# Summing four of eight factor slices by accumulating DMAs in the last two setup steps of a cross-attention and FFN kernel

## The chip, the cores and the metric

The kernel runs on one core of one Trainium2 chip. The metric is the device time of one execution, in microseconds (us); lower is better. The five engines are TensorE (PE in the profile), VectorE (DVE), ScalarE (ACT), GpSimd (POOL) and SyncE (SP); each works through its own queue in order, and they wait for one another by semaphores.

## The reference

The input `x` has 8 sequences of 1024 rows with 1024 elements, all in float32. Each sequence has 64 memory rows and a mask over them. There are eight factor matrices of 1024x1024.

```python
x = x + attention(layernorm(x), memory, mask)      # one head, 64 memory rows per sequence
mixed = einsum('btd,rde->bte', layernorm(x), factors)   # sums over the 8 factors r too
x = x + mixed / sqrt(8) + bias
```

The sum over `r` doesn't depend on `x`, so the eight factors can be added up once, and the second line is then one product with a single 1024x1024 matrix.

## The kernel before

**Work per group.** The 8192 rows are handled in 16 groups of 512 rows. A group's rows are loaded (`load_rows`, L140, and from group 2 on `load_blocks`, L131, for a blocked copy that VectorE transposes), scored against the memory (`scores`, `scores_back`, `softmax`, `weights_back`, `read_out`), added to `x` (`residual`, L292), normalised (`norm_stats`, `normalize`), transposed, and multiplied by the summed factor matrix. A group has two halves `q`, each with seven `unit`s or `product`s: the matrix product is done with seven block products instead of eight, on combined blocks of the rows (`combine_rows`) and of the matrix (`combine_factors`). Each product is four matmuls of 128x512 (L398), and `give` (L411) adds its result to `x`.

**The combined matrix.** The blocks are kept in seven tiles, `b11`, `t2`, `b22`, `b21`, `t1`, `t3`, `t4`. The raw sums are made in `QUADS` order: steps 0 and 1 sum the top half of the matrix into `b11` and `t2`, steps 2 and 3 the bottom half into `b21` and `b22`. `combine_factors` then forms `t1` (steps 0, 1), and `t2`, `t3` (L445, L446) and `t4` (L448) in steps 2 and 3. The units need `b11`, `t1`, `t2`, `b22`, `t3`, `b21`, `t4` in this order, so units 0 and 1 can run after step 1, and unit 2 and all that follow need the whole of steps 2 and 3.

**A step.** One step takes a quarter of each of the eight factors, a slice of 128 partitions by 2048 elements, 1 MB. SP issues the loads (`load_factor`, L428) into tiles of the pool `big`, which has nine buffers of 8 KB per partition. The same pool holds the transposed rows (`xT`, `hT`), the normalised rows (`h`) and the blocked copies (`xb`, `hb`). VectorE adds some of the slices into the block tiles (L540); TensorE adds the others, by multiplying them with the identity into four PSUM banks (`sum_on_pe`, L436), and VectorE adds those banks at the end of the step (L547). In steps 0 and 1 VectorE takes factors 0 to 3 and TensorE 4 to 7; in steps 2 and 3 VectorE takes 0 to 4 and TensorE 5, 6 and 7.

**What runs beside the steps.** `beside(step, turn)` writes out by hand which work of groups 0 and 1 stands between the turns of each step. Around the change these are, in this order: in step 2 the transposes of group 0's second half and `unit(0, 0, 0)`; `unit(0, 0, 1)`; the transposes of group 1 (`transpose_x_pe`, L193 and L194) with `row_sums(1)` (L147 on ScalarE, then `nmean`, L149 on GpSimd); more transposes with `row_squares(1)` (L158 on ScalarE, which needs `nmean`, then L162 and L163 on GpSimd). In step 3 they are `scores(1)`, `scores_back(1)`, `softmax(1)` with `unit(0, 1, 0)`, and `unit(0, 1, 1)`. GpSimd's queue thus holds small arithmetic only, among it L305 to L309 of `norm_stats`. The schedule is the program's order: nothing reorders an engine's queue.

Of the kernel before, what the change touches and what calls it, by code (L numbers as in the profile page):

```python
# [12 lines left out]
ALU = mybir.AluOpType  # L13
# [7 lines left out]
def kernel(  # L21
# [18 lines left out]
    nc = tc.nc  # L40
# [7 lines left out]
    NC = DA // Q  # L48
    KH = NC // 2
    H = D // 2  # L50
# [17 lines left out]
    COMMON = ["ps0", "ps1", "ps2", "ps3"]  # L68
    ring = list(COMMON)

    def bank(name: str, tag: str = ""):
        if not tag:
            ring.append(ring.pop(0))
            tag = ring[-1]
        return psum.tile([P, 512], F32, tag=tag, name=name)

    def big_tile(shape, name: str):
        return big.tile(shape, F32, tag="big", name=name)
# [346 lines left out]
    def load_factor(step: int, r: int):  # L425

        f = big_tile([P, 2, D], f"f_{step}_{r}")
        nc.sync.dma_start(  # L428
            f, factors[r].rearrange("(p c) e -> p c e", c=NC)[:, 2 * step : 2 * step + 2, :]
        )  # L430
        return f

    def sum_on_pe(f, first: bool, last: bool, banks):
        for c in range(2):
            for n in range(2):
                nc.tensor.matmul(banks[c, n], ident, f[:, c, ts(n, H)], start=first, stop=last)  # L436

    def combine_factors(step: int, n: int):

        c = slice(2 * (step % 2), 2 * (step % 2) + 2)  # L440
        w = {key: tile[:, c, :] for key, tile in wq.items()}
        if step < 2 and n == 0:
            nc.vector.tensor_sub(w["t1"], w["t2"], w["b11"])
        if step >= 2 and n == 1:
            nc.vector.tensor_sub(w["t2"], w["b22"], w["t1"])  # L445
            nc.vector.tensor_sub(w["t3"], w["t2"], w["b11"])  # L446
        if step >= 2 and n == 0:
            nc.vector.tensor_sub(w["t4"], w["b21"], w["t2"])  # L448
# [17 lines left out]
    def beside(i: int, s: int):  # L466
        if (i, s) == (0, -1):
            centre_memory(0)
            row_stats(0)
            transpose_x_pe(0, 0)  # L470
            transpose_x_pe(0, 1)
        if (i, s) == (0, 0):
            transpose_memory(0)
            scores(0)
        if (i, s) == (0, 1):
            scores_back(0)
        if (i, s) == (0, 2):
            softmax(0)
            nc.scalar.dma_start(bias_bc, bias.partition_broadcast(P))
        if (i, s) == (0, 3):  # L480
            weights_back(0)
        if (i, s) == (1, 0):
            read_out(0, 0)
            residual(0, 0)
        if (i, s) == (1, 1):
            norm_stats(0, 0)
            read_out(0, 1)
            normalize(0, 0, False)
            residual(0, 1)
        if (i, s) == (1, 2):  # L490
            norm_stats(0, 1)
            transpose_h_pe(0, 0)
            load_rows(1, nc.sync)
        if (i, s) == (1, 3):
            normalize(0, 1, False)
            add_bias(0, 0, nc.vector)
        if (i, s) == (2, 0):
            transpose_h_pe(0, 1)
            combine_rows(0, 0)
            unit(0, 0, 0)  # L500
        if (i, s) == (2, 1):
            unit(0, 0, 1)
            add_bias(0, 1, nc.vector)
        if (i, s) == (2, 2):
            combine_rows(0, 1, (1,))
            transpose_x_pe(1, 0)
            row_sums(1)
        if (i, s) == (2, 3):
            transpose_x_pe(1, 1)
            row_squares(1)  # L510
        if (i, s) == (3, 0):
            scores(1)
        if (i, s) == (3, 1):
            scores_back(1)
        if (i, s) == (3, 2):
            softmax(1)
            unit(0, 1, 0)
        if (i, s) == (3, 3):
            unit(0, 1, 1)

    for step in range(NS):
        c2 = slice(2 * (step % 2), 2 * (step % 2) + 2)
        w2 = [wq[key][:, c2, :] for key in QUADS[step // 2]]

        sums = {(c, n): bank(f"sum_{step}_{c}_{n}", COMMON[2 * c + n]) for c in range(2) for n in range(2)}
        ring[:] = ["u0", "v0", "u1", "v1"] if step < 2 else ["u1", "v1"]
        beside(step, -1)

        turns = [((0,), 4), ((1,), 5), ((2,), 6), ((3,), 7)]
        if step >= 2:  # L530
            turns = [((0, 1), None), ((2,), 5), ((3,), 6), ((4,), 7)]
        before = None
        for s, (mine, other) in enumerate(turns):
            for r in mine:
                f = load_factor(step, r)
                if r == 0:
                    before = f
                    continue
                for n, w in enumerate(w2):
                    nc.vector.tensor_add(w, before[:, :, ts(n, H)] if r == 1 else w, f[:, :, ts(n, H)])  # L540
            if other is not None:
                fp = load_factor(step, other)
                sum_on_pe(fp, other == turns[1][1] - (step < 2), other == 7, sums)
            beside(step, s)
        for n in (1, 0):
            for c in range(2):
                nc.vector.tensor_add(w2[n][:, c, :], sums[c, n], w2[n][:, c, :])  # L547
            combine_factors(step, n)
    ring[:] = COMMON

# [42 lines left out]
    for g in range(1, NG):  # L593
        n, m = g + 1, g + 2
# [91 lines left out]
```

## Time and profile before

| | us |
|---|---|
| median of 3 runs | 1019.69 |
| lowest and highest | 1014.05 and 1020.04 |
| the profiled execution | 1018.94 |
| its span, first to last instruction | 1016.6 |
| TensorE busy | 985.7 |
| VectorE busy | 669.3 |
| ScalarE busy | 349.6 |
| GpSimd busy | 215.8 |

The profile covers one execution. Times in its views are counted from the start of the span. A line such as L436 is a line of the kernel file before the change. A float32 matmul is recorded as two entries, so four matmuls show as x8. The chain of waits gives, for each piece, its start, its length, and what it is; the chain is followed back from the last instruction. In the windows each engine has its busy time and count, then come TensorE's clock, DMA's share of the 16 engines and GB/s. The bracket at the end of a timeline row tells how long the engine was idle ahead of it and what ended that.

### The profile page before, as it was taken

Reading aid. Unit: us, or ns where it says so; the run is one execution under the profiler, and the core shown is the slowest. Engines: PE = TensorE matmul, PEld = TensorE weight load, DVE = VectorE, ACT = ScalarE, POOL = GpSimd, SP = SyncE. Lnnn points to the kernel's source line nnn. Section 1 sums busy time; section 2 is a strip of 40 time slices with the busy share of each in tenths; the row PEclk is TensorE's granted clock in tenths of the full one; section 3 lists DMA queues with packets and bytes.
Section 4 is the critical chain, followed back from the end, with each engine's and each line's share of the span. In section 5 each row is a group of like instructions: output and inputs, shape, how many; then the busy total and the mean of one; then the engine's idle time right before and its main releaser. Section 6 shows DMA issues by size and latency. Waiting matters only on the chain.

```text
span 1016.6 us, 8902 instructions
## 1 busy us (share of the span) xinstructions
PE 985.7 (97%) x2896; PEld 443.4 (44%) x2896; DVE 669.3 (66%) x895; ACT 349.6 (34%) x521; POOL 215.8 (21%) x250
## 2 busy tenths in 40 slices
PE   4979999999999999999999999999999999999998
PEld 3445344444444444444444444444444444444443
DVE  3598577675758575675758575675758575695531
ACT  2135134432625143432625143432625143430300
POOL 0020012222213040222213040222213040240400
PEclk9999999999999999999999999999999999999999
DMA  9996936455573937455573837356573837340321
GB/s 320 418 407 267 285 88 164 144 138 149 143 210 95 229 99 166 138 144 143 145 207 95 213 116 171 133 142 146 142 209 92 213 120 171 131 123 32 90 85 41
DMA packets 93517, 166.86 MB, mean 164 GB/s; under 512 B 12320, under 2 KB 71840, under 8 KB 89376
## 3 DMA queue, kind: packets, MB, share of 16 engines
q1 hardware_dynamic: 93024, 165.20, 56.6%
q10 hardware_dynamic: 448, 1.11, 0.4%
q8 instruction: 22, 0.36, 0.1%
q14 instruction: 23, 0.19, 0.1%
HBM read 101.25 MB, written 33.55 MB: 133 GB/s over the span
## 4 chain that ended last, share of the span: by engine, by line
PE 93%; DVE 2%; DMA 2%; ACT 1%; POOL 1%; issue 0%; ACTq 0%
PE yu L398 43%; PE yv L398 22%; PE yz L398 11%; PE ro L281 6%; PE scT L218 5%; PE sum L436 4%; DMA f<-in_L_ffn_factors_dram 2%; PE memTp L120 1%; DVE st L302 1%; DMA mask_raw<-in_mask_BxS_bk_dram 1%; PE tp L193 1%; DVE x L292 0%; ACT junk L158 0%; ACT h L321 0%; PE eTp L269 0%
## 5 line engine op out<-in xcount | busy, mean ns | idle before, releaser
L398 PE MATMUL yu<-t,hT 128*128 128x512 f32 x512 | 232.2, 596 | 0.0
L321 ACT ACTIVATE h<-x,nb,rstd 128x1024 f32<-128x1024 f32 x64 | 137.4, 2198 | 233.0 <-POOL nb L309 167.8
L411 DVE SCALAR_TENSOR_TENSOR x<-yu,x 128x512 f32<-128x512 f32 x128 | 88.0, 687 | 161.8 <-PE yu L398 161.7
L398 PEld LDWEIGHTS yu<-t,hT 128*128 128x128 f32 x512 | 96.5, 191 | 117.0 <-issue 116.2
L333 POOL TENSOR_TENSOR x<-x,bias_bc 128x1024 f32<-128x1024 f32 x60 | 141.8, 2388 | 0.0
L398 PE MATMUL yz<-b,hT 128*128 128x512 f32 x256 | 117.2, 600 | 0.0
L398 PE MATMUL yu<-t,s 128*128 128x512 f32 x256 | 115.4, 593 | 1.5 <-DVE t L445 1.5
L398 PE MATMUL yu<-b,hT 128*128 128x512 f32 x256 | 116.5, 598 | 0.0
L398 PE MATMUL yv<-t,s 128*128 128x512 f32 x256 | 116.5, 598 | 0.0
L398 PE MATMUL yv<-b,s 128*128 128x512 f32 x256 | 115.1, 592 | 0.0
L182 DVE STREAM_TRANSPOSE xT<-xb 128x2048 f32<-128x2048 f32 x28 | 109.8, 3922 | 0.0
L411 DVE SCALAR_TENSOR_TENSOR x<-yv,x 128x512 f32<-128x512 f32 x64 | 43.8, 684 | 93.7 <-PE yv L398 93.7
L292 DVE SCALAR_TENSOR_TENSOR x<-ro,rden,x 128x512 f32<-128x512 f32 x128 | 87.2, 744 | 13.5 <-PE ro L281 13.5
L149 POOL TENSOR_SCALAR nmean<-sum 128x4 f32<-128x4 f32 x15 | 3.6, 237 | 397.9 <-ACT junk L147 397.9
L302 DVE BATCH_NORM_STATS2 st<-x 128x6 f32<-128x512 f32 x128 | 80.3, 669 | 0.0
L398 PEld LDWEIGHTS yu<-b,hT 128*128 128x128 f32 x256 | 47.4, 190 | 64.7 <-issue 64.2
L398 PEld LDWEIGHTS yv<-b,s 128*128 128x128 f32 x256 | 48.6, 190 | 60.7 <-issue 60.5
L398 PEld LDWEIGHTS yz<-b,hT 128*128 128x128 f32 x256 | 47.0, 190 | 63.4 <-issue 51.7
L398 PEld LDWEIGHTS yv<-t,s 128*128 128x128 f32 x256 | 47.5, 190 | 59.9 <-issue 57.6
L398 PEld LDWEIGHTS yu<-t,s 128*128 128x128 f32 x256 | 47.5, 190 | 56.4 <-issue 54.0
L347 DVE STREAM_TRANSPOSE hT<-hb 128x1024 f32<-128x1024 f32 x60 | 70.9, 1219 | 0.2
L158 ACT ACTIVATE junk<-x,nmean 128x1024 f32<-128x1024 f32 x60 | 68.8, 1147 | 1.5
(72 smaller groups left out, 783.7 us busy)
## 6 DMA issues: line engine op xcount, KB each, us to landing
x<-in_x_dram SPq DMA_DIRECT2D x64, 512.0 KB, 10.3
f<-in_L_ffn_factors_dram SPq DMA_DIRECT2D x32, 1024.0 KB, 12.0
out_dram<-x SPq DMA_DIRECT2D x64, 512.0 KB, 2.9
hb<-h SPq DMA_DIRECT2D x480, 64.0 KB, 2.0
xb<-in_x_dram SPq DMA_DIRECT2D x112, 256.0 KB, 7.8
mem<-in_ctx_dram SPq DMA_DIRECT2D x14, 256.0 KB, 3.9
mem<-in_ctx_dram ACTq DMA_DIRECT2D x2, 256.0 KB, 10.3
bias_bc<-in_L_ffn_bias_dram ACTq DMA_DIRECT2D x1, 512.0 KB, 8.1
```

Of the source, the lines that this page charges most:

```text
L158: nc.scalar.activation(junk, st["x", g, t], AF.Square, bias=nmean[:, t : t + 1], accum_out=ss[:, t : t + 1])
L182: nc.vector.transpose(xT.rearrange("p c (t j) -> p t c j", j=Q), xb.rearrange("p t (i c) -> p t c i", i=Q))
L218: nc.tensor.matmul(ps[ts(h, M), : 2 * P], mT[:, c, :], st["xb", g, h][:, c, :], start=(c == 0), stop=(c == NC - 1),)
L281: nc.tensor.matmul(ps, eT[ts(h, M), q, :], m[ts(h, M), ts(n, H)], start=True, stop=True)
L292: nc.vector.scalar_tensor_tensor(xt, st.pop(("ro", g, q, n, h)), rden[:, k : k + 1], xt, ALU.mult, ALU.add)
L302: nc.vector.bn_stats(stats[:, n, :], xt[:, ts(n, H)])
L321: nc.scalar.activation(dst, src, AF.Identity, bias=nb[:, h : h + 1], scale=rstd[:, h : h + 1],)
L333: eng.tensor_add(xt, xt, bias_bc)
L347: nc.vector.transpose(hT[:, h].rearrange("p c (t j) -> p t c j", j=Q), hb[:, h].rearrange("p t (c i) -> p t c i", i=Q),)
L398: nc.tensor.matmul(ps, lhs[:, c, :], wq[rhs][:, c, :], start=(first and c == 0), stop=(c == KH - 1), skip_group_check=True,)
L411: nc.vector.scalar_tensor_tensor(xt, st["y", g, q, key], ISR, xt, ALU.mult, ALU.add)
L436: nc.tensor.matmul(banks[c, n], ident, f[:, c, ts(n, H)], start=first, stop=last)
```

## The change

In steps 2 and 3 SP first loads factor 4 into a tile. GpSimd issues three DMAs that add factors 5, 6 and 7 to that tile in place, each waiting for the one before. SP loads factors 0 to 3, which VectorE adds as before, and at the end of the step VectorE adds the accumulated tile to each block (L563 of the changed file). TensorE adds nothing in these two steps, and they take no PSUM banks for sums. Steps 0 and 1 stay as they were. A step's big tiles go from eight to five. The order of loads changes too: factor 4, then 0, 1, 2, 3.

```diff
+    def add_factor(f, step: int, r: int):
+        nc.gpsimd.dma_start(
+            f,
+            factors[r].rearrange("(p c) e -> p c e", c=NC)[:, 2 * step : 2 * step + 2, :],
+            accum_op=ALU.add,
+        )
...
-        turns = [((0,), 4), ((1,), 5), ((2,), 6), ((3,), 7)]
         if step >= 2:
-            turns = [((0, 1), None), ((2,), 5), ((3,), 6), ((4,), 7)]
+            fp = load_factor(step, 4)
         before = None
-        for s, (mine, other) in enumerate(turns):
-            for r in mine:
-                f = load_factor(step, r)
-                if r == 0:
-                    before = f
-                    continue
-                for n, w in enumerate(w2):
-                    nc.vector.tensor_add(w, before[:, :, ts(n, H)] if r == 1 else w, f[:, :, ts(n, H)])
-            if other is not None:
-                fp = load_factor(step, other)
-                sum_on_pe(fp, other == turns[1][1] - (step < 2), other == 7, sums)
+        for s in range(4):
+            if step >= 2 and s < 3:
+                add_factor(fp, step, 5 + s)
+            f = load_factor(step, s)
+            if step < 2:
+                fp = load_factor(step, 4 + s)
+                sum_on_pe(fp, s == 0, s == 3, sums)
+            for n, w in enumerate(w2):
+                if s > 0:
+                    nc.vector.tensor_add(w, w if before is None else before[:, :, ts(n, H)], f[:, :, ts(n, H)])
+            before = f if s == 0 else None
             beside(step, s)
         for n in (1, 0):
-            for c in range(2):
-                nc.vector.tensor_add(w2[n][:, c, :], sums[c, n], w2[n][:, c, :])
+            if step < 2:
+                for c in range(2):
+                    nc.vector.tensor_add(w2[n][:, c, :], sums[c, n], w2[n][:, c, :])
+            else:
+                nc.vector.tensor_add(w2[n], w2[n], fp[:, :, ts(n, H)])
             combine_factors(step, n)
```

In the changed file L445, L446 and L448 of `combine_factors` stand at L453, L454 and L456. Other lines are named as they stand before.

More of the change, by code (lines that the diff above doesn't have):

```diff
@@ L523 @@
         w2 = [wq[key][:, c2, :] for key in QUADS[step // 2]]
-        sums = {(c, n): bank(f"sum_{step}_{c}_{n}", COMMON[2 * c + n]) for c in range(2) for n in range(2)}
+        if step < 2:
+            sums = {
+                (c, n): bank(f"sum_{step}_{c}_{n}", COMMON[2 * c + n])
+                for c in range(2)
+                for n in range(2)
+            }
         ring[:] = ["u0", "v0", "u1", "v1"] if step < 2 else ["u1", "v1"]
         beside(step, -1)
-        turns = [((0,), 4), ((1,), 5), ((2,), 6), ((3,), 7)]
         if step >= 2:
-            turns = [((0, 1), None), ((2,), 5), ((3,), 6), ((4,), 7)]
+            fp = load_factor(step, 4)
         before = None
-        for s, (mine, other) in enumerate(turns):
-            for r in mine:
-                f = load_factor(step, r)
-                if r == 0:
-                    before = f
-                    continue
-                for n, w in enumerate(w2):
-                    nc.vector.tensor_add(w, before[:, :, ts(n, H)] if r == 1 else w, f[:, :, ts(n, H)])
-            if other is not None:
-                fp = load_factor(step, other)
-                sum_on_pe(fp, other == turns[1][1] - (step < 2), other == 7, sums)
+        for s in range(4):
[9 more added lines that the diff above has]
+            before = f if s == 0 else None
             beside(step, s)
         for n in (1, 0):
-            for c in range(2):
-                nc.vector.tensor_add(w2[n][:, c, :], sums[c, n], w2[n][:, c, :])
+            if step < 2:
+                for c in range(2):
+                    nc.vector.tensor_add(w2[n][:, c, :], sums[c, n], w2[n][:, c, :])
+            else:
+                nc.vector.tensor_add(w2[n], w2[n], fp[:, :, ts(n, H)])
             combine_factors(step, n)
```

## Prediction

> **What bounds the kernel now.** I read the page first: the busy rows, the forty slices, and the DMA row under them.
>
> ```profile
> PE 985.7 (97%) x2896; PEld 443.4 (44%) x2896; DVE 669.3 (66%) x895; ACT 349.6 (34%) x521; POOL 215.8 (21%) x250
> PE   4979999999999999999999999999999999999998
> PEclk9999999999999999999999999999999999999999
> DMA  9996936455573937455573837356573837340321
> ```
>
> TensorE is full except in the first four slices; a slice is 25.4 us. The changed steps lie in slices three to five, about 64 to 122 us. After that TensorE sets the pace, so whatever the change does to the moment when the last combined factor is ready goes through one for one to the end. Next I read the chain of waits in the first 200 us, to find that moment.
>
> ```profile
> 74.90 3.43 PE sum L436 x8
> 81.77 3.43 PE sum L436 x8
> 87.58 3.45 PE sum L436 x8
> 100.13 4.75 DMA f<-in_L_ffn_factors_dram
> 104.92 3.70 PE sum L436 x8
> 112.06 3.43 PE sum L436 x8
> 118.96 0.69 DVE x L411
> 119.65 1.21 DVE b L547 x2
> 120.88 1.24 DVE t L445
> 122.16 1.98 PE yu L398 x4
> ```
>
> At 122.16 TensorE starts the first product that needs `t2` (unit 2 of group 0), which DVE finishes when all eight factors of step 3 are in. Call this moment T; the forecast is 1018.94 us plus the move of T. Third, the windows show how full DMA is (second last column the share, last GB/s), and the timeline of GpSimd shows where its queue is free.
>
> ```profile
> 60.00:70.00 10.00, 5.63 (x17) 3.14 (x18) 9.90 (x14) 3.50 (x5) 4.25 (x4) 0.88 1.01 421
> 70.00:80.00 10.00, 10.00 (x30) 5.08 (x30) 8.04 (x10) 1.66 (x3) 0.00 (x0) 0.95 0.96 369
> 80.00:90.00 10.00, 9.72 (x36) 5.22 (x35) 8.10 (x8) 3.92 (x7) 0.00 (x0) 1.00 0.64 242
> ...
> 65.67 1.08 POOL L309 TENSOR_SCALAR nb<-nb 128x2 f32<-128x2 f32 x1
> 92.87 0.23 POOL L149 TENSOR_SCALAR nmean<-sum 128x4 f32<-128x4 f32 x1 [26.12 <-ACT junk L147]
> 100.18 1.17 POOL L162 TENSOR_SCALAR rs<-ss 128x4 f32<-128x4 f32 x1 [7.08 <-ACT junk L158]
> 101.44 1.85 POOL L163 TENSOR_TENSOR rs<-rs,neghalf 128x4 f32<-128x4 f32 x1
> ...
> DMA to landing us min/median/max: 4.6/12.0/18.3
> ```
>
> At 421 GB/s a 1.05 MB factor slice passes in 2.5 us; a lone load takes 4.6 us from issue to landing (the minimum in the last line), so about 2.1 us of it is fixed. DMA is full to nearly 80 us and has gaps later, when SP waits for buffers.
>
> **What the Trainium skill says.** "DMA: Bandwidth & Descriptors", SWDGE vs HWDGE vs iDMA: only GpSimd can issue an accumulating DMA, by software on its cores, and issuing engines share the same 16 DMA engines. Its Rules for kernel authors say that an accumulate must wait for the earlier DMA's semaphore: so three accumulates into one tile are a chain, landing after landing. "Collectives: The Full Stack", The bandwidth ceiling: a reducing transfer reads two sources through one read ring and ran at half the rate of a copy. "SBUF — State Buffer", Who interferes with whom: a DVE instruction with two SBUF inputs contends with GpSimd's reads. The trace has no DMA from GpSimd, so shows none of the first three; it agrees with the last: L305 took 0.24 us at 54.57 and 1.08 us at 62.25, beside DVE's adds.
>
> **What the change removes.** In the compiled order 24 matmuls of `sum` go, six groups of 3.43 us: 20.6 us of TensorE's time ahead of T. That is the most that can be gained. DVE loses eight 128x512 additions from PSUM (about 0.68 us each) but takes 128x1024 ones as before; the end of a step is L563 (`t2`'s half of the sum), L453, L454, L563, L456, five of 1.22 us. Two of these, 2.5 us, stand between the last accumulate's landing and T, against L547 twice and L445, also 2.5 us (119.65 to 122.12). Five instead of eight buffers a step let SP load ahead.
>
> **What it adds: the price D of one accumulate, issue to landing.** A lone load's 4.6 us, plus 2.5 us if the second source read halves the rate, plus about 1 us for software emission. For the last, the skill gives first bytes of 1 us against 0.6 us ("DMA: Bandwidth & Descriptors", Specifications), and I add 0.6 for the slowing seen at L305. D is 8.1 us undisturbed. The bounds: 4.6 if the second read and the emission are free; 13 if the emission or the adder is several times dearer. It cannot be below 4.6, as it moves no fewer bytes than a load. Sharing with SP's loads adds up to 2.5 us per MB passing meanwhile.
>
> **What moves, step 2.** L309 ends on GpSimd at 66.75, and factor 4 has landed: a load lands at 60.96 (where the last `sum` group of step 1 starts), so factors 4, 0, 1, 2, 3 land at about 63.4, 65.9, 68.4, 70.9, 73.4. First accumulate: issued 66.8, with 4.5 us of SP's loads still queued: 66.8 + 8.1 + 4.5 = 79.4. Second: SP's next two loads (step 3's factors 4 and 0) are released by DVE's adds of factors 0 and 1, at about 78.1; of their 5 us I charge 4: 79.4 + 8.1 + 4 = 91.5. Third: issued at 91.5, lands, with 1 us of sharing, at 100.6. GpSimd's queue is in order, so `nmean` (L149) stands behind the third issue: about 92.8.
>
> TensorE meanwhile is early. Without the sums, product `yv` ends at 78.2 and group 1's transposes start there, not at 85.04: 6.9 us earlier. ScalarE's squares (L158, from 95.04 before) could start at 88.2, but wait for `nmean` until 92.8. Four of them take 5.1 us, L162 and L163 3.1 us: 101.0. `scT`'s copy on ScalarE, and so `sc` and the products behind it, wait with the squares; those products end near 105, still ahead of T.
>
> **Step 3.** Its first accumulate stands behind L163 on GpSimd: 101.0. The step's own last load (factor 3) waits for step 2's accumulated tile, read by DVE near 105.5; `xb` and `x` of group 2 (4 MB) follow. So the three run beside transfers: 101.0 + 8.1 + 1.4 = 110.5; + 8.1 + 3.9 = 122.5 (half of the eight `xb` pieces' some 9 us is charged); + 8.1 + 2 = 132.6. DVE adds 2.5: T = 135.1 against 122.16, +12.9 us. TensorE's saved 20.6 us becomes idle time in front of T, about 30 us of it. What comes after T is unchanged: `xb` and `x` land at about their old time or a few us later, while the work that needs them moved back by 13 us. Sum: 1018.94 + 12.9 = 1031.8, taken as 1032. The profiled execution is 0.75 us under the median of 1019.69, which is nothing here.
>
> T moves by about five times what D does: three accumulates of step 3, and two of step 2 through `nmean`. D of 7 gives 1026, 9 gives 1036, 10 gives 1041.
>
> **Rivals.** (A) The accumulate runs at a copy's price. At D = 4.6 the first two land at 76 and about 82, `nmean` is never late, step 3 starts at 96.3 (88.2 + 5.1 + 3.1, rounded) and T is 96.3 + 13.8 + 3 of sharing + 2.5 = 115.6: 1012. This is the case that is not slower. It decides below D = 6.2, where 96.3 + 18.6 + 4.7 + 2.5 is 122.1. For it: DMA has room after 80 us (share 0.64 and less). Against it: two reads, and emission in software beside DVE's adds. (B) The accumulate is far dearer, D of 11 to 15: emission starved while DVE runs its adds, or an adder below half rate. T moves by 5 x 2.9 more at D = 11, 5 x 6.9 at D = 15: 1046 to 1066. For it: L305, L306 and L309 stretched two- to fivefold beside DVE in this very stretch. Against it: the stretched rows are arithmetic that reads SBUF, while the engines' data path is not DVE's. (C) That the change does nothing of the kind: out, since the compiled order has the six DMAs on GpSimd's queue and no `sum` in steps 2 and 3.
>
> **How the numbers follow.** The forecast (D from 7 to 10) has 0.45, A 0.2, B 0.35. A measurement of this kernel can tell about 1%, 10 us, from no change. Faster by more needs T before 112, so D under 3.4, below its bound: 0.04 for what the sum misses. Of the forecast's share a fifth (D under 7.5) and nearly all of A's lie within 1%: 0.26. The rest, 0.70, is slower. The range takes A from D = 5.5 up and B to D = 13: 1015 to 1056.
>
> **What would show it.** Right: accumulates landing 8 to 12 us after their issue, `nmean` near 93, L163 near 101, no `sum` after 66 us, a TensorE gap of tens of us that ends with DVE's L453 near 135, DVE waiting for the accumulate ahead of L563. The D step is wrong if landings come 5 to 6 us after issue; the gating step is wrong if L163 ends near 96 although D is 8. The whole is wrong if T is set by something else: SP's loads, or DVE still adding factors 0 to 3.

## The result and the profile after

| | before | after |
|---|---|---|
| median, us | 1019.57 of 4 runs | 1034.14 of 4 runs |
| lowest and highest, us | 1014.05 to 1020.04 | 1032.54 to 1035.48 |
| the profiled execution, us | 1018.94 | 1034.63 |
| its span, us | 1016.6 | 1032.9 |
| T, us from the span's start | 122.16 | 135.62 |
| from T to the span's end, us | 894.4 | 897.3 |

The changed kernel is slower by a factor of 1.0155 (95% interval 1.0117 to 1.0193). The span grew by 16.3 us: 13.5 us ahead of T and 2.9 us behind it. The page of the changed kernel, its busy row and three rows of the forty slices (25.8 us each now), shows the place:

```profile
PE 972.5 (94%) x2848; PEld 437.7 (42%) x2848; DVE 664.4 (64%) x887; ACT 349.9 (34%) x521; POOL 219.7 (21%) x256
PE   5975379999999999999999999999999999999998
PEclk9998779999999999999999999999999999999999
DMA  9999925838373655638382755637482746540321
```

T is where the second half of unit 2's product starts: its row has x4, two of the four matmuls. The first two read the part of `t2` that step 2 made, and had run earlier (at 118.76 us before, at 117.71 after); the prediction, which calls T the start of the product, missed that, but not the wait.

TensorE is busy 13.2 us less, and the digits 5 and 3 in slices four and five (77 to 129 us) say that the time went into idling. The clock row has dropped to 8 and 7 there. DMA is full for five slices instead of four. The chain of waits between 65 and 136 us (start, length, what) names the cause:

```profile
65.07 12.25 DMA f<-in_L_ffn_factors_dram
...
77.62 12.61 DMA f<-in_L_ffn_factors_dram
...
90.52 0.86 POOL f L435
91.37 0.29 POOL nmean L149
...
97.15 0.09 POOL rs L163
...
98.16 8.23 DMA f<-in_L_ffn_factors_dram
...
106.69 13.09 DMA f<-in_L_ffn_factors_dram
...
120.06 12.93 DMA f<-in_L_ffn_factors_dram
...
133.09 1.24 DVE b L563
134.34 1.23 DVE t L453
...
135.62 3.78 PE yu L398 x4
```

Before, this stretch was mostly TensorE's `sum` groups. Now it is accumulates on GpSimd's queue, one after the other. The fourth (the first of step 3, at 98.16) took 8.23 us; the others took 12 to 13 us, but the third, of which the chain shows only the issue at 90.52, had landed when VectorE went on at 100.08, so within 9.5 us. Between the third and the fourth stand `nmean`, the four squares on ScalarE and L162 and L163, as GpSimd's queue is in order. The waits of that stretch (who waited for what: us in total, times, longest) show who paid:

```profile
POOL f L435 <- DMA f<-in_L_ffn_factors_dram: 43.6, 4, 12.5
DVE b L563 <- DMA f<-in_L_ffn_factors_dram: 30.3, 2, 15.8
PE yu L398 <- DVE t L453: 16.0, 1, 16.0
ACT junk L158 <- POOL nmean L149: 4.9, 1, 4.9
```

VectorE stood twice in front of the accumulated tile, 15.8 us at the end of step 2 and 14.5 us at the end of step 3; TensorE idled 16.0 us ahead of T. The windows (second last column DMA's share, the one before it TensorE's clock) show what the accumulates ran beside; the last line is of the kernel before:

```profile
60.00:70.00 10.00, 6.80 (x27) 3.87 (x28) 9.90 (x13) 4.40 (x6) 5.28 (x5) 1.00 1.01 409
80.00:90.00 10.00, 5.82 (x28) 3.78 (x30) 4.26 (x5) 5.69 (x12) 0.00 (x0) 0.66 1.02 291
110.00:120.00 10.00, 8.44 (x12) 3.28 (x12) 5.50 (x8) 1.44 (x8) 0.00 (x0) 0.64 1.02 216
120.00:130.00 10.00, 0.00 (x0) 0.00 (x0) 0.00 (x0) 0.00 (x0) 0.86 (x1) 0.70 1.09 242
130.00:140.00 10.00, 4.38 (x7) 2.17 (x8) 6.68 (x7) 0.13 (x1) 0.00 (x0) 0.50 0.50 165
```

```profile
110.00:120.00 10.00, 10.00 (x24) 4.37 (x23) 4.00 (x5) 0.00 (x0) 0.00 (x0) 1.00 1.11 215
```

Read share and GB/s together (the view's shares can pass 1; take that as full): from 80 to 90 us the engines are as full at 291 GB/s as they were at 409, with accumulates and factor loads alone. From 110 to 130 the loads of group 2 (`xb` issued from 105.4, `x` from 116.1) pass through them too, and these also fill the engines at few bytes: before the change, without any accumulate, the share was 1.11 at 215 GB/s while they passed. On average the share is 0.88 before (windows from 60 to 120 us) and 0.98 after (60 to 130).

### The profile page after: what moved, and what is told of

It is laid out like the page before. It is cut to its first block, busy times and chain, and to the rows that moved or that the text cites. A ratio compares the mean times of both kernels' runs of the same rounds, so it can differ in the third digit from the quotient of the medians.

```text
span 1032.9 us, 8796 instructions
## 1 busy us (share of the span) xinstructions
PE 972.5 (94%) x2848; PEld 437.7 (42%) x2848; DVE 664.4 (64%) x887; ACT 349.9 (34%) x521; POOL 219.7 (21%) x256
## 3 DMA queue, kind: packets, MB, share of 16 engines
q10 hardware_dynamic: 448, 1.11, 0.4%
## 4 chain that ended last, share of the span: by engine, by line
PE 88%; DMA 7%; DVE 2%; ACT 1%; issue 1%; POOL 1%; POOLq 0%; DVEq 0%
PE yu L398 42%; PE yv L398 21%; PE yz L398 11%; DMA f<-in_L_ffn_factors_dram 7%; PE ro L281 6%; PE scT L218 5%; PE sum L444 2%; PE memTp L120 1%; DVE st L302 1%; DMA mask_raw<-in_mask_BxS_bk_dram 1%; ACT junk L158 0%; DVE x L292 0%; PE eTp L269 0%; PE sc L234 0%; POOL rstd L306 0%
## 5 line engine op out<-in xcount | busy, mean ns | idle before, releaser
L398 PEld LDWEIGHTS yu<-t,hT 128*128 128x128 f32 x512 | 96.6, 191 | 117.0 <-issue 116.1
L398 PE MATMUL yv<-t,s 128*128 128x512 f32 x256 | 119.7, 611 | 8.7 <-DVE sm L243 8.7
L292 DVE SCALAR_TENSOR_TENSOR x<-ro,rden,x 128x512 f32<-128x512 f32 x128 | 87.2, 743 | 13.5 <-PE ro L281 13.5
## 6 DMA issues: line engine op xcount, KB each, us to landing
f<-in_L_ffn_factors_dram SPq DMA_DIRECT2D x26, 1024.0 KB, 13.5
```

Source lines behind the costliest of these rows:

```text
L292: nc.vector.scalar_tensor_tensor(xt, st.pop(("ro", g, q, n, h)), rden[:, k : k + 1], xt, ALU.mult, ALU.add)
L398: nc.tensor.matmul(ps, lhs[:, c, :], wq[rhs][:, c, :], start=(first and c == 0), stop=(c == KH - 1), skip_group_check=True,)
```

## The experiments

Each kernel is the changed one with one edit (e4 joins two; e6, e7 and e9 keep the change in one step alone), measured beside the kernel before; ratios are to that one, with a 95% interval. A line number is that of the kernel named, so one line can bear different numbers. The theory is the prediction's: a chain of landings, gated by GpSimd's queue. The rival that took its place in part is that the 16 DMA engines lack time for accumulates and loads together, so that starting earlier gains nothing.

| kernel | median us (runs) | ratio | T | T to end |
|---|---|---|---|---|
| e1_plain | 1024.57 (6) | 1.008 [1.005, 1.0109] | 125.99 | 895.9 |
| e2_queue | 1033.37 (4) | 1.0145 [1.0114, 1.0176] | 136.46 | 897.2 |
| e3_pairs | 1016.94 (20) | 0.9984 [0.9972, 0.9997] | 119.82 | 894.3 |
| e4_pairs_queue | 1020.38 (20) | 1.0016 [1.0003, 1.0028] | 123.52 | 896.1 |
| e5_defer | 1029.88 (4) | 1.0124 [1.0104, 1.0144] | 127.33 | 901.0 |
| e6_step2 | 1030.11 (4) | 1.0125 [1.0103, 1.0148] | 134.19 | 894.7 |
| e7_step3 | 1036.90 (4) | 1.0198 [1.0174, 1.0223] | 136.99 | 896.6 |
| e8_warm | 1033.13 (4) | 1.0158 [1.0136, 1.018] | 136.48 | 894.4 |
| e9_pairs2 | 1017.81 (12) | 0.9996 [0.9981, 1.001] | 121.21 | 894.5 |
| e10_single | 1018.26 (20) | 0.9997 [0.9984, 1.001] | 122.66 | 897.5 |

The last column is the span less T. It differs by at most 3.1 us from before's 894.4 in all but e5, so a kernel's time is T's.

### e1_plain: GpSimd's DMAs copy, and don't add

```diff
             factors[r].rearrange("(p c) e -> p c e", c=NC)[:, 2 * step : 2 * step + 2, :],
-            accum_op=ALU.add,
```

> The changed kernel, but GpSimd's six DMAs only copy: they overwrite the tile instead of adding to it, so factors 4, 5 and 6 are left out of the bottom half of the sum. The waits and the queue are those of the changed kernel. Theory (half of an accumulate's data time is the second source read): a copy of step 3 that meets no other traffic lands 5.6 to 6 us after its issue instead of 8.2, T comes at 120 to 125 instead of 135.6, the time is 1017 to 1023 us. Rival (the price is in GpSimd's software path and the chain of waits, not in the adding): a lone copy still takes 8 us, and the time stays within 3 us of 1034.

The chain of e1 in step 3:

```profile
97.21 11.38 DMA f<-in_L_ffn_factors_dram
...
108.88 9.25 DMA f<-in_L_ffn_factors_dram
...
118.41 4.95 DMA f<-in_L_ffn_factors_dram
```

The last copy, once the loads are through, takes 4.95 us, less than expected, and the second of step 2 about 4.9. A lone accumulate is 8.2 us, so accumulating costs 3.3 us more than copying, and a copy issued from GpSimd costs only 0.3 us over a lone load of 4.6. T came to 125.99 and the time to 1024.57, just above what was expected; the first two copies still run beside group 2's loads, and took 11.4 and 9.3 us. The page's DMA rows, first of the changed kernel and then of e1 (packets, MB, share of the 16 engines over the span), price the adding a second time:

```profile
q0 software_dynamic: 864, 6.29, 3.1%
```

```profile
q0 software_dynamic: 864, 6.29, 1.6%
```

The same bytes in the same packets: 3.1% of 1032.9 us over six DMAs is 5.3 us of all 16 engines for an accumulate, 1.6% of 1021.9 us is 2.7 us for a copy. Six of them take some 16 us more engine time. From 61 to 133 us the share is 0.98 in the changed kernel and 0.78 in e1. The copies alone, chained and sharing, still cost 0.8%.

### e2_queue: step 3's first accumulate goes ahead of the squares' end

```diff
             transpose_x_pe(1, 1)
-            row_squares(1)
 ...
         if (i, s) == (3, 0):
+            row_squares(1)
```

> The changed kernel with row_squares(1) one turn later, so that the first accumulate of step 3 stands ahead of L162 and L163 on GpSimd's queue. Theory (that queue holds back step 3's chain): its first accumulate is issued near 91.5 instead of 98.2, beside the third of step 2, and T comes 4 to 6 us earlier: 1028 to 1030 us. Rival (the DMA engines are what is short, so an earlier issue only shares them longer): the landings of step 3 move by less than 1 us, 1033 to 1035.

The chain of e2:

```profile
91.03 16.13 DMA f<-in_L_ffn_factors_dram
...
107.44 12.10 DMA f<-in_L_ffn_factors_dram
...
119.83 14.00 DMA f<-in_L_ffn_factors_dram
```

The theory fell. The accumulate was issued 7.1 us earlier and landed 0.8 us later, at 107.16 against 106.40: it took 16.1 us, now beside the last accumulate of step 2 and step 3's loads. T stayed (136.46). Waiting behind L163 was real, but it was not what set the end; the rival holds.

### e3_pairs: two tiles with one accumulate each

```diff
         if step >= 2:
-            fp = load_factor(step, 4)
+            fp, fq = load_factor(step, 4), load_factor(step, 6)
+            add_factor(fp, step, 5)
+            add_factor(fq, step, 7)
 ...
-            if step >= 2 and s < 3:
-                add_factor(fp, step, 5 + s)
 ...
-                nc.vector.tensor_add(w2[n], w2[n], fp[:, :, ts(n, H)])
+                for f in (fp, fq):
+                    nc.vector.tensor_add(w2[n], w2[n], f[:, :, ts(n, H)])
```

The three chained accumulates of each step become two independent ones and one more load; TensorE adds nothing here either.

> Two accumulates a step into two tiles (factor 5 into 4, factor 7 into 6), issued one after the other with no wait between them; VectorE adds both tiles at the end; six loads on SP. Theory (landing after landing is what costs): the chain of three becomes one, nmean is on time, step 3's pair is issued near 96 and has landed by 111, T is 113 to 116, and the time 1010 to 1014 us. Rival (bytes through the DMA engines cost, the chain does not): as much is moved less two second reads, so T falls by 5 us or less, 1028 to 1032.

T fell by 15.8 us to 119.82, where one accumulate fewer in each step, taken as engine time alone, was put at 5 us or less; so the chain cost. The kernel is just faster than before: 0.9984, an interval that leaves out 1 by little. It missed the 1010 to 1014 expected. From 100 to 120 us the engines are full (share 1.02, then 1.08), and the last link of its chain is now a plain load of SP's,

```profile
95.32 17.81 DMA f<-in_L_ffn_factors_dram
...
113.15 1.35 DVE b L555 x2
```

a slice that would take 4.6 us alone and took 17.8.

### e4_pairs_queue: the pairs and e2's edit together

> The two changes before together: pairs, and row_squares(1) behind step 3's accumulates. Theory: step 3's pair is issued by 86, lands by 103, T is 104 to 109 and the time 1002 to 1007 us, under both kernels. Rival (DMA bytes): no better than the pairs alone by more than 1 us.

Missed, in the wrong direction: T is 3.7 us later than in e3. VectorE's first add of step 3, in e3 and then in e4 (the bracket is its wait):

```profile
99.24 2.36 DVE L555 TENSOR_TENSOR b<-f,f 128x1024 f32<-128x1024 f32 x2 [2.34 <-DMA f<-in_L_ffn_factors_dram]
```

```profile
106.35 2.36 DVE L555 TENSOR_TENSOR b<-f,f 128x1024 f32<-128x1024 f32 x2 [9.07 <-DMA f<-in_L_ffn_factors_dram]
```

With the accumulates issued earlier, the first of SP's factors that VectorE adds in this step came 7 us later. From 90 to 100 us the accumulates filled engine time that e3 had left idle (share 0.97 instead of 0.71), and still the loads came later. How this makes up the 3.7 us of T isn't followed further.

### e5_defer: group 2's loads after the gap

```diff
-    load_blocks(2, nc.sync)
-    load_rows(2, nc.sync)
 ...
         if k == 0:
             weights_back(1)
+            load_rows(2, nc.scalar)
+            load_blocks(2, nc.scalar)
```

> The changed kernel, with the loads of group 2 (xb and x, 4 MB) taken from SP's queue and issued by ScalarE after weights_back(1), so behind T. Theory (the second and third accumulate of step 3 take 13 us instead of 8.2 because they wait behind these loads on the DMA engines): the second, behind factor 3 alone, lands at about 118, the third takes 8.2 us and lands near 126.5, T is 129 instead of 135.6; the time is about 1027 us if the later loads cost nothing, more if they do. Rival (the chain of three into one tile is slow by itself): both still take 12 to 13 us, T stays within 1 us.

The chain of e5:

```profile
96.96 9.81 DMA f<-in_L_ffn_factors_dram
...
107.06 9.23 DMA f<-in_L_ffn_factors_dram
...
116.58 8.12 DMA f<-in_L_ffn_factors_dram
...
144.97 5.89 DMA out_dram<-x
```

Without the 4.2 MB of `xb` and `x`, the second and third accumulate of step 3 took 9.2 and 8.1 us instead of 13.1 and 12.9, and T came 8.3 us earlier, 1.2 us of it because the first was issued earlier. So the sharing charged in the prediction is real. The time gained less: ScalarE reaches the loads only at 131.6, and 3.7 us of the gain was lost behind T, where the chain now runs through a store and the row sums of the late `x`. The best place for these loads wasn't searched for.

### e6_step2 and e7_step3: accumulates in one of the two steps

```diff
-        if step < 2:
+        if step != 2:        # e7: step != 3
             sums = {...}
 ...
+        if step == 2:        # e7: step == 3; the other step as before the change
```

> Accumulates in step 2 alone; step 3 sums as before the change. Theory (step 2's chain is late, but what waits for it has slack, and step 3's chain sets T): T between 119 and 124, 1017 to 1022 us. Rival (the two steps cost alike): half of the 14 us, 1026 us.

> Accumulates in step 3 alone; step 2 sums as before the change. Theory: TensorE is as late in step 2 as before the change, so L163 ends at about 103 and the first accumulate is issued there, 5 us later than in the changed kernel; with the loads of group 2 ahead of it, T is 138 to 142 and the time 1036 to 1041 us: one step of the change alone costs more than both. Rival (the two steps cost alike): 1026 us.

e6 was expected near the time before and came to 1030. Step 2's accumulates don't touch `t2` through step 3's chain here, as there is none, yet T moved by 12 us. VectorE's timeline and the chain of e6:

```profile
101.86 1.23 DVE L569 TENSOR_TENSOR b<-b,f 128x1024 f32<-128x1024 f32 x1 [14.22 <-DMA f<-in_L_ffn_factors_dram]
```

```profile
105.60 1.15 DVE b L569
...
107.19 6.81 DMA f<-in_L_ffn_factors_dram
...
114.04 6.62 PE sum L444 x8
120.66 3.43 PE yu L398 x8
124.09 3.43 PE sum L444 x8
```

VectorE was held 14.2 us for the accumulated tile, and a buffer came free only at 106.8. SP's last four loads of step 3 stood behind it and landed from 111.6 to 119.0, while the engines had been mostly idle (share 0.30 from 100 to 110 us), and TensorE's sums came last. A chain in step 2 thus costs by a road that the prediction hadn't: VectorE's queue and the buffers it frees.

e7's time is in the range expected, its T (136.99) 1 us below it. One step alone costs at least as much as both; that it costs more isn't clear of the noise (1.0198 and 1.0155, with intervals that overlap). TensorE's sums in step 2 held the squares back, L163 ended at 103.4 instead of 98.2, and step 3's chain started there:

```profile
103.39 14.25 DMA f<-in_L_ffn_factors_dram
...
117.94 8.17 DMA f<-in_L_ffn_factors_dram
...
126.39 7.97 DMA f<-in_L_ffn_factors_dram
```

The last two, with group 2's loads gone from about 121 us on, give D three times over with the lone one above: 8.0 to 8.2 us. So three accumulates in a row would take about 25 us from issue to landing even on quiet engines, by these figures.

### e8_warm: fifteen matmuls in TensorE's gap

```diff
         if (i, s) == (3, 3):
             unit(0, 1, 1)
+            idle = bank("idle", "ps0")
+            for k in range(15):
+                nc.tensor.matmul(idle, ident, wq["b11"][:, 0, :], start=True, stop=True)
```

> The changed kernel, with 15 matmuls that nobody reads between unit(0, 1, 1) and unit(0, 0, 2), in TensorE's gap ahead of T. Theory (T moved by 13.5 us, and the rest of the profiled span's 16.3 comes from matmuls right after the gap at a lower granted clock): T stays, the first matmuls after it take 1.9 instead of 3.8 us, the span is shorter by 2 to 2.8 us, about 1031.5 us. Rival (the rest lies elsewhere): no change beyond 0.5 us.

TensorE's timeline, first of the changed kernel and then of e8:

```profile
135.62 3.78 PE L398 MATMUL yu<-t,s 128*128 128x512 f32 x4 [16.03 <-DVE t L453]
139.62 4.37 PE L398 MATMUL yv<-b,s 128*128 128x512 f32 x8
```

```profile
117.56 13.04 PE L530 MATMUL idle<-b,ident 128*128 128x512 f32 x30
136.48 3.62 PE L398 MATMUL yu<-t,s 128*128 128x512 f32 x4 [4.17 <-DVE t L453]
140.16 3.60 PE L398 MATMUL yv<-b,s 128*128 128x512 f32 x8
```

With the gap cut to 4.2 us, T to the end is 894.4 us, as before the change, against 897.3. The half product after the gap stayed slow (3.62 us, where 1.98 was before and 1.9 expected), the next product is back at 3.60. From T to the `ro` row behind these products it is 5.73 us before, 8.30 in the changed kernel and 7.21 in e8: 2.6 of the 2.9 us lie here, and e8 wins back 1.1 of them. The rest of what e8 gains behind T lies elsewhere and isn't explained. All this is one span of each kernel; the two times, 1033.13 and 1034.14, don't tell them apart.

### e9_pairs2: the pairs in step 2 alone

> Two accumulates into two tiles in step 2 alone; step 3 as before the change. It tells why accumulates in step 2 alone had cost 12 us. Theory (the chain landed at 101.8, VectorE stood in its queue for 14 us until then, and the last four loads of step 3 waited for the tile it frees at 106.8): the pair lands by 87, VectorE waits 3 us at most, the last load of step 3 lands at 108 to 112 and T is 120 to 125, 1016 to 1021 us. Rival (only the DMA engines' time counts): one accumulate and one load's difference less, so some 3 to 5 us less than with the chain, 1025 to 1027 us.

As expected. VectorE's timeline at the end of step 2, where e6 waited 14.2 us:

```profile
85.26 2.35 DVE L559 TENSOR_TENSOR b<-b,f 128x1024 f32<-128x1024 f32 x2
87.65 2.49 DVE L570 TENSOR_TENSOR b<-b,f 128x1024 f32<-128x1024 f32 x2
```

There is no bracket, so no wait: both tiles had landed when L570 started at 87.65. The step, the engine and the operation are those of e6; what is gone is the chain of three. One accumulate fewer, as engine time, was put at 3 to 5 us; T came 13.0 us earlier.

### e10_single: one accumulate a step, the other two slices on TensorE

```diff
-        if step < 2:
+        if True:
             sums = {...}
 ...
         if step >= 2:
             fp = load_factor(step, 4)
+            add_factor(fp, step, 5)
 ...
+            elif s in (1, 2):
+                sum_on_pe(load_factor(step, 5 + s), s == 1, s == 2, sums)
```

> One accumulate a step (factor 5 into 4), factors 6 and 7 summed on TensorE as before the change, 0 to 3 on VectorE, in steps 2 and 3. Theory (what costs is the chain of landings and the DMA engines' time, 5.3 us an accumulate against 2.5 a load; what is gained is TensorE's 3.4 us a sum): no landing waits for another, DMA takes 5.6 us more in all and TensorE 6.9 us less, T between 116 and 122, 1013 to 1019 us. Rival (an accumulate delays the step whatever its number): T is 125 or later, 1022 us or more.

The time is within what was expected, T (122.66) just above it, and the time is no different from before. The accumulate of step 3 in the chain, and VectorE's wait for it:

```profile
104.70 14.00 DMA f<-in_L_ffn_factors_dram
```

```profile
118.80 1.23 DVE L561 TENSOR_TENSOR b<-b,f 128x1024 f32<-128x1024 f32 x1 [1.47 <-DMA f<-in_L_ffn_factors_dram]
```

It stood behind L163 and took 14.0 us beside loads. With a third of its additions gone, TensorE reached the half product ahead of T 2.3 us earlier than before (116.43 against 118.76); VectorE's wait of 1.47 us and its one more addition of 1.24 us took that back.

## Why the prediction was right, and where its steps were not

**The bound, right.** What moves T moves the end one for one, in ten kernels, but for up to 3.1 us (6.6 in e5).

**The price D: right.** D was put at 8.1 us and is 8.0 to 8.2. It was built as 4.6 for the load, 2.5 for the second read and about 1 for software. By e1 a copy's issue from GpSimd costs 0.3 us and accumulating 3.3 more, of which 2.6 is engine time. Whether the other 0.7 us is software isn't shown; GpSimd's issuing instruction is 0.3 us longer with the adding. The Trainium skill, "Collectives: The Full Stack", The bandwidth ceiling, says that a reducing transfer ran at half a copy's rate; 5.3 against 2.7 us of engine time agrees.

**Step 2, right within 3 us.** Forecast landings 79.4, 91.5 and 100.6; seen 77.3, 90.2 and 100.0. `nmean` was forecast at 92.8 and started on the chain at 91.4; L163 forecast to end at 101.0, seen at 98.2.

**Step 3, right in sum, with the sharing misplaced.** Forecast landings 110.5, 122.5 and 132.6; seen 106.4, 119.8 and 133.0. The first was issued 2.8 us earlier than forecast and ran nearly alone; the second and third paid 4.9 and 4.7 us of sharing where 3.9 and 2 were charged. The errors cancel, so it is in part luck that T, forecast at 135.1, is 135.62. TensorE's idle time, forecast as one gap of about 30 us, came as 16.0 us ahead of T and shorter gaps before.

**"T moves by about five times what D does": not borne out.** It rested on the first accumulate of step 3 waiting for the squares behind `nmean`. That wait was there, but it cost little: in e1, where `nmean` is never late, the first DMA of step 3 is issued at 97.21, only 0.95 us earlier, and in e2, which issues it 7.1 us earlier, T doesn't come earlier. e1 gives the factor: D falls by 3.3 us and T by 9.6, about three times.

**Sharing, under-priced.** What the sum treated as a small addition, "up to 2.5 us per MB passing meanwhile", is the second limit: an accumulate holds the engines for 5.3 us, where a load holds them 2.5. With sixteen slices in steps 2 and 3, six of them accumulated, engine time grows from 40 us to some 57 (an estimate from these two figures), in a stretch where the share is 0.88 on average already. The room that rival A claims, "share 0.64 and less" after 80 us, was misread: before the change the share is 0.64, 0.68, 0.88 and 1.11 from 80 to 120 us. The loads put off in e5 relieve the engines and leave the accumulates as they are, and T falls by 8.3 us; the copies of e1 relieve them and shorten the chain as well, so its 9.6 us can't be divided between the two. An earlier issue relieves nothing. Nor is it the engines alone: e7 has three accumulates fewer and room on the engines (share 0.84 from 61 to 137 us), and its T is no earlier, by the chain.

**"What comes after T is unchanged": off by 2.9 us.** TensorE ran slow after its gap (clock 0.50 in the window from 130 to 140), and 2.6 of the 2.9 us lie in the first products behind it. e8's span behind T is that of before, but filling the gap shows only 1.1 us of this in those products. With the half microsecond by which T was missed this makes up the 16.3 us of the span against the forecast 12.9.

**The rivals.** A, a copy's price, is out at D of 8.2; and e1 shows that even at that price the kernel would be slower, as its three copies of step 3 paid some 11 us of sharing, where A's estimate of T at 115.6 has 3. B, a far dearer accumulate, is out: undisturbed ones take 8 us, and the one of 8.23 us ran beside VectorE's adds from 100.08 on. The 12 to 16 us are seen only beside other transfers. C is out.

**Open.** Why an accumulate loses so much beside loads (16.1 us in e2), as their order on each engine isn't seen; how the 13.5 us divide between the chain and the full engines; and e8's saving, in the time itself and by its place.

## What to carry to other kernels

Accumulating DMAs into one tile were a serial chain here, at 8 us for each megabyte, and each took twice a load's time on the DMA engines; independent tiles with one accumulate apiece, four accumulates in place of six, turned a loss of 1.5% into a gain of 0.2%. Before moving additions from a compute engine to DMA, look at DMA's share in that very stage: here it was 0.88 and went to 0.98, and TensorE, relieved of its additions, waited for what relieved it. An earlier issue gained nothing (e2) and held up the loads (e4).

## What was not expected of the hardware

The issue from GpSimd added only 0.3 us to a lone 1 MB copy (4.95 against 4.6 us), although its issuing instruction is on the queue for 0.5 to 0.8 us, and 0.9 to 1.1 us with the adding. And TensorE's clock, as the windows give it, fell to 0.50 after a gap of 16 us: the half product at T took 3.78 us instead of 1.98. A short gap did nearly as much: the same two matmuls took 1.98 us after a gap of 1.5 us (before, e6, e9), 2.48 after 2.7 us (e4), and 3.62 to 3.78 after 3.7 to 4.4 us (e3, e8, e10).
